# Cross attention's query and output projections as seven products of quarters, in an encoder-decoder kernel

## The chip, the core and the metric

The kernel runs on one core of a Trainium2 chip. The time is device microseconds of one launch. Everything is float32. Engines are called by the profile's names: PE (TensorE matmul), PEld (its weight loads), DVE (VectorE), ACT (ScalarE), POOL (GpSimd), SP (SyncE, which issues the transfers).

## What is computed

One layer of an encoder and a decoder, for a batch of 2. The source has 77 rows of 512 features, the target 2048; there are 16 heads of 32 and 2048 hidden features. The encoder's part is small. The decoder is:

```
yn = ln(y, n1);  y = y + mha(yn, yn, sa, causal and relative bias)
y = y + mha(ln(y, n2), memory, ca, relative bias)        # 77 keys
h = ln(y, n3);   y = y + relu(h @ ff1.T + b1) @ ff2.T + b2

mha:  q = (xq @ wq.T + bq);  k, v likewise from the other side, in 16 heads
      out = softmax(q k.T / sqrt(32) + bias) v;  return out @ w_out.T + b_out
```

The cross attention (`ca`) has two products with a 512 x 512 matrix on the target's side: the query projection and the output projection.

## The kernel before

The target's rows are worked in eight blocks of 512 (four per batch element), each of four tiles of 128 rows. There are three phases.

*Attention phase* (up to about 1740 us): self-attention in 128 units (batch, block, group of heads, tile). Small work is hung on lists by unit number: `light[n]` and `late[n]` hold functions that are called in unit n's slot. There the sums of the feed-forward's weights are prepared too (`w1_sums`, `w2_sums`): four loads of quarters into a scratch region `free`, sums and differences on POOL (`minus`, L1113), and a store into DRAM tensors `w1_d` and `w2_d`. The first block's cross attention (`first_cross`) is also hung there.

*Feed-forward with cross attention*: an outer loop over the eight blocks, x = 0 to 7. A block's feed-forward has `per` = 56 slots (`ff_slot`): 28 for the first matrix (`first_product`, matmuls at L1326, four of 128x256 per slot) and 28 for the second (`second_product`, matmuls at L1355, two products of four 128x128 matmuls per slot, and one in every fourth slot). Both matrices are already multiplied as seven products of quarters in place of eight: `ONE` and `TWO` list which left operand (a quarter or one of the sums S1 to S4) meets which right operand (a quarter or T1 to T4), into which of two accumulating chains of PSUM banks, and to which quarter of the result the chain's content then goes. The operand sums are made on the chip: `sums_n` makes T1 to T4 of the normalised input on POOL, all in slot 0; `sums_h` makes those of the hidden layer, on DVE (L1275, L1113, L1293) and POOL, four slots ahead of their use. Weight tiles of 256 KB stream through a ring of 16 (`w_ring`), which `feed` refills at the end of each slot; `next_w` takes the next tile.

Between the slots of block x-1's feed-forward stands the cross attention of block x (`cross(x)`, x = 1 to 7). It is a generator: `plan[n]` lists the steps of slot n, and before each `ff_slot` the loop calls `next(side)`. So the order on every engine is written out by hand: in each slot first the cross steps, then the feed-forward's.

The cross steps before, for tile t of a block:

- `norm_stages` n2: statistics in slot t (DVE, then POOL L767, L768), centring in t+2 (ACT L774; then POOL adds the output bias row to the residual y, L775), turning by PE in t+4 (L780), with ACT writing the scaled result (L783) into `nT2`.
- `q_group` in slots 9 to 12: 4 groups of 4 matmuls of 128x512 (L790) with weights resident in `w_q`, evacuated by DVE with bias and scale (L791).
- `attend_stages` at slot 14 + 7t: scores (L805, four banks, then on DVE a maximum L814 and a subtraction L815 for each bank, and with a relative bias an addition L812 before them), exponential 2 slots later (ACT L818), row sums (DVE L823) and normalising (POOL L829) 3 later, turning of the probabilities 6 later (16 transposes, L835, four banks; ACT copies L836), times values 9 later (L843; ACT copies to SBUF, L847), output projection 11 later (4 matmuls of 128x512, L852, and a DVE addition to y, L853). The first tile of a block starts one slot earlier.
- `norm_stages` n3, at 13, 15 and 17 slots after the tile's start, as above with the feed-forward's bias row.

Banks 0 to 3 of PSUM belong to the cross steps, in rotation (`bank()`); banks 4 to 7 are the feed-forward's chains (`pairs`).

*The last block's feed-forward* has no cross steps beside it.

Of the kernel before, what the change touches and what calls it, by code (L numbers as in the profile page):

```python
# [17 lines left out]
P = 128  # L18
# [36 lines left out]
def tile_encoder_decoder(ctx: ExitStack, tc: tile.TileContext, ins, out):  # L55
# [13 lines left out]
    make_identity(nc, ident)  # L69
    mhalf = const.tile([P, TB], F32, name="mhalf")  # L70
    nc.gpsimd.memset(mhalf, -0.5)
    vecs = const.tile([P, NVEC], F32, name="vecs")
# [85 lines left out]
    with (  # L158
# [597 lines left out]
        def norm_stages(y, n, row, place, done):  # L756
# [14 lines left out]
            def center():  # L771
                xn = keep["xn"] = place()
                rs = keep["rs"]
                nc.scalar.activation(xn, y(), AF.Identity, bias=rs[:, 2:3], scale=rs[:, 1:2])  # L774
                nc.gpsimd.tensor_tensor(y(), y(), row, ALU.add)  # L775

# [7 lines left out]

            return stats, center, turned

# [6 lines left out]
        def attend_stages(q, kTc, v, y, biased, pr, pts, place, w_o, bi=None):  # L793
# [44 lines left out]
            def times_v():  # L838
                ot = bank()
                for g in range(NC):  # L840
                    for r in range(HC):
                        h = g * HC + r
                        nc.tensor.matmul(  # L843
                            ot[rows4(r), ts(g, P)], v[:, ts(h, HD)], pts(g)[:, ts(r, P)], start=True, stop=True
                        )
                keep["oT"] = place()
                nc.scalar.copy(keep["oT"], ot)  # L847
# [6 lines left out]

            return score, exp, sums, normalize, turned, times_v, out

        def first_cross():
# [41 lines left out]
            for t in range(TB):  # L899
# [3 lines left out]
                )  # L903
                for k, f in enumerate(fs):
                    at(1 + t + k, f)
            for g in range(NC):
                at(7 + g, lambda g=g: q_group(g, wq[:, :, ts(g, P)], nT, qT[:, g, :]))
            for t in range(TB):
                y = lambda t=t: ys[t]
                fs = attend_stages(  # L910
                    lambda g, t=t: qT[:, g, ts(t, P)], kTc, vc, y, t < 2, prs[t % 2], pts, lambda: oT, wo
                )
# [3 lines left out]
                for k, f in enumerate(fs):  # L916
                    at(18 + 3 * t + k, f)
# [130 lines left out]
        oflat = oT_all.rearrange("p a q -> p (a q)")  # L1048
        pr = oflat[:, : H * S]
        kTcs = [pts_all[:, 4 + b, : NC * S].rearrange("p (c k) -> p c k", k=S) for b in range(B)]  # L1050
        w_q, vcs, qT = [], [], []

# [13 lines left out]
        def early_loads():  # L1066
            nc.sync.dma_start(nTt, nT3_d)
            row_into(bv, "dec_ca_out_b")
            for o in range(2):
                w_q.append(small_w(o * P, "dec_ca_in_wT"))  # L1070
            w_q.append(pts_all[:, 6, :].rearrange("p (c o) -> p c o", c=NC))

        def last_loads():
            t = sb.tile([P, MB], F32, name="q", tag="q", bufs=3)
            t = t.rearrange("p (c o) -> p c o", c=NC)
            nc.sync.dma_start(t, wchunk("dec_ca_in_wT", (NC - 1) * P, P))
            w_q.append(t)
            for b in range(B):
                t = sb.tile([P, MB], F32, name="q", tag="q", bufs=3)
                nc.sync.dma_start(t[:S, :], cv_d[:, b, :])  # L1080
                vcs.append(t)

        def late_loads():
            nc.sync.dma_start(w_q[2], wchunk("dec_ca_in_wT", 2 * P, P))
            for t in range(TB):
                new_y(1, t)
            for b in range(B):
                nc.sync.dma_start(kTcs[b], ckT_d[:, :, ts(b, S)])
            for _ in range(2):
                t = sb.tile([P, HC, 2 * P], F32, name="bias", tag="bias", bufs=2)  # L1090
                qT.append(t.rearrange("p (g a) k -> p g (a k)", g=2))

        light[len(units) - 5].append(early_loads)
        light[len(units) - 1].append(last_loads)


# [4 lines left out]
        w1_d = dram.tile([4, NC, P, D], F32, name="w1_d")  # L1101
        w2_d = dram.tile([7, 7, P, D], F32, name="w2_d")
        free = pp[:, 3 * HC * MB : END - 3 * HC * MB]
        tens = free.rearrange("p (z q o) -> p z q o", z=8, q=2)
# [56 lines left out]
        def w1_store(n):  # L1161
            nc.sync.dma_start(
                w1_d[:, n].rearrange("s p x -> p s x"), free[:, 4 * D :].rearrange("p (s x) -> p s x", s=4)
            )

        u = 2 * NU
        for c, k in enumerate((0, 2, 4, 10)):
# [37 lines left out]
        def w1_tile(name, n):  # L1205
# [4 lines left out]
            return ins["dec_ff1_wT"][c * TOK : (c + 1) * TOK, o : o + TOK].rearrange("(c p) o -> p c o", p=P)  # L1210

        def weight_tiles():
            for x in range(len(blocks)):
                for j, n in first_slots:
                    yield w1_tile(ONE[j][0], n)
                for _, name, _, _, _ in TWO:
                    for k in range(7):
                        yield w2_d[ON_W2[name], k]

# [27 lines left out]

        def sums_n():
            minus(gp, of_n("T1"), of_n("12"), of_n("11"))
            minus(gp, of_n("T2"), of_n("22"), of_n("T1"))  # L1250
            minus(gp, of_n("T3"), of_n("22"), of_n("12"))
            minus(gp, of_n("T4"), of_n("21"), of_n("T2"))

# [92 lines left out]
        def second_product(x, j, part):  # L1346
# [37 lines left out]
            elif done:  # L1384
                after[x * per + FIRST + 4 * j + 3 + 3] = store

        def ff_slot(s):
            x, n = divmod(s, per)
            if n == 0:
                sums_n()  # L1390
            k = n - FIRST + 4
# [10 lines left out]

        xt_ring, xt_turn = [pts_all[:, 7, :]], [0]

# [4 lines left out]
        def cross(x):  # L1409
# [9 lines left out]
            for t in range(TB):  # L1419
                fs = norm_stages(  # L1420
                    lambda t=t: y_of(x, t), "n2", bv, place("xt"), lambda t=t: nT2[:, :, ts(t, P)]
                )
                for k, f in zip((0, 2, 4), fs):
                    plan[t + k].append(f)
            for g in range(NC):
                plan[9 + g].append(lambda g=g: q_group(g, w_q[g], nT2, qT[g // 2][:, g % 2, :]))
            bias_1 = None
            if m == 0:

                spare = [pts_all[:, 4, :], vcs[0], y_of(x + 1, 0), y_of(x + 1, 1)]  # L1430
                bias_1 = [a[:, : NC * S].rearrange("p (g k) -> p g k", k=S) for a in spare]
                plan[3].append(lambda: bias_tile(pr.rearrange("p (h k) -> p h k", k=S), 2, P, S, 255))
                plan[5].append(lambda: [bias_tile(a, 2, P, S, 255 - P, r, HC) for r, a in enumerate(bias_1)])
            for t in range(TB):
                at = 14 + 7 * t
                y = lambda t=t: y_of(x, t)
                biased = m == 0 and t < 2
                fs = attend_stages(
                    lambda g, t=t: qT[g // 2][:, g % 2, ts(t, P)], kTcs[b], vcs[b][:S, :], y, biased, pr,
                    lambda g: pts_all[:S, g, :], place("xr"), wbt,  # L1440
                    bias_1 if biased and t else None,
                )
# [129 lines left out]
```

## Time and profile before

| | us |
|---|---|
| three runs, median (lowest to highest) | 2850.07 (2849.39 to 2850.22) |
| the profiled execution | 2851.01 |
| its span, from first to last instruction | 2849.2 |
| busy: PE, DVE, ACT, POOL | 2800.5, 1888.1, 1370.0, 836.7 |
| one block of the last phase with its cross attention (2340.20 to 2482.76) | 142.56 |

Views used below: the page's busy shares; the list of waits (who waited for whom: total us, number of times, longest); groups of instructions by line (count, busy time in all, mean ns of one); the timeline (start, length, engine, line, operation, out<-in, shape, count, and in brackets the idle time ahead of it and what ended it); the chain of work that ended last (start, length, engine, line, count); and busy time by windows. The length of a matmul record reaches into the next one, so the pace of a stream is read from the starts.

### The profile page before, as it was taken

The numbers are of one execution on the slowest core, as the hardware profiler recorded it, in microseconds if no ns is written. First come the engines' busy times: TensorE is split into PE (matmuls) and PEld (weight loads), VectorE is DVE, ScalarE is ACT, GpSimd is POOL, SyncE is SP. The second block draws the span as 40 slices with busy tenths as digits, with TensorE's granted clock in tenths as the row PEclk, the third lists the DMA queues.
The fourth block names the chain that finished last, engine by engine and source line by source line (L and its number), as shares of the span: only waits on it lengthen the run. The fifth ranks groups of instructions, "written<-read, shape, count | busy, mean of one in ns | idle before, by whom it ended". The sixth has DMA issues, their size and how long they took to land. (4 is left out here: it accounts for less than half of the span.)

```text
span 2849.2 us, 64689 instructions
## 1 busy us (share of the span) xinstructions
PE 2800.5 (98%) x25662; PEld 2020.5 (71%) x25662; DVE 1888.1 (66%) x5366; ACT 1370.0 (48%) x2583; POOL 836.7 (29%) x695
## 2 busy tenths in 40 slices
PE   9899999999999999999999999999999999999998
PEld 5557666666666456666666677888888888888888
DVE  4766687878886578788778894545454645454545
ACT  3444465546665446555556674333333333333331
POOL 0301143300100302121100002363636363636355
PEclk9899999999999999999999999999999999999999
DMA  6414343401112512232301115454546454545465
GB/s 172 123 46 140 119 140 106 129 23 49 36 50 65 141 39 71 81 106 78 98 20 43 44 34 191 137 178 135 180 136 197 134 181 135 180 135 180 120 203 181
DMA packets 262336, 324.55 MB, mean 114 GB/s; under 512 B 36192, under 2 KB 149392, under 8 KB 261906
## 3 DMA queue, kind: packets, MB, share of 16 engines
q1 hardware_dynamic: 262034, 320.42, 37.4%
q8 instruction: 202, 3.31, 0.5%
q14 instruction: 100, 0.82, 0.1%
HBM read 280.94 MB, written 39.40 MB: 112 GB/s over the span
## 5 line engine op out<-in xcount | busy, mean ns | idle before, releaser
L403 ACT ACTIVATE pp<-pp,nm 128x128 f32<-128x128 f32 (+15 forms) x512 | 611.7, 1201 | 258.9 <-DVE nm L398 258.6
L381 DVE TENSOR_SCALAR_CACHE_REDUCE pp<-psum 128x512 f32<-128x512 f32 (+3 forms) x1024 | 559.6, 591 | 63.1 <-PE psum L372 61.2
L426 PEld LDWEIGHTS psum<-ident,pp 128*128 128x128 f32 x4352 | 475.1, 142 | 106.2 <-DVE pp L381 50.8
L426 PE MATMUL psum<-ident,pp 128*128 128x128 f32 x4352 | 535.0, 278 | 7.0 <-ACT pp L403 3.7
L432 ACT COPY pts<-psum 128x512 f32<-128x512 f32 (+3 forms) x592 | 297.3, 575 | 457.3 <-PE psum L426 343.5
L430 DVE COPY pts<-psum 128x512 f32<-128x512 f32 (+2 forms) x544 | 330.0, 660 | 66.7 <-PE psum L426 66.3
L372 PE MATMUL psum<-kT,q 32*128 32x512 f32 (+3 forms) x2560 | 359.9, 576 | 5.2 <-ACT pts L432 2.6
L443 PEld LDWEIGHTS psum<-pts,vv 128*32 128x32 f32 x8704 | 226.2, 110 | 124.5 <-issue 116.6
L1355 PE MATMUL psum<-pp 128*128 128x128 f32 x2560 | 306.4, 276 | 1.9 <-POOL pp L1113 1.6
L1355 PEld LDWEIGHTS psum<-pp 128*128 128x128 f32 x2560 | 295.8, 192 | 17.4 <-issue 12.6
L443 PE MATMUL psum<-pts,vv 128*32 128x128 f32 x8704 | 279.4, 276 | 0.7 <-ACT pts L432 0.5
L1326 PE MATMUL psum<-vv,pp 128*128 128x256 f32 x1024 | 238.5, 381 | 0.0
L372 PEld LDWEIGHTS psum<-kT,q 32*128 32x128 f32 x2560 | 124.7, 183 | 141.5 <-issue 89.6
L1326 PEld LDWEIGHTS psum<-vv,pp 128*128 128x128 f32 x1024 | 189.8, 190 | 32.2 <-issue 8.4
L388 DVE CUSTOM_DVE_ANT_0 pp<-psum,bias 128x256 f32<-128x256 f32 (+1 forms) x512 | 196.0, 411 | 16.7 <-PE psum L372 16.5
L1113 POOL TENSOR_TENSOR pp<-pp 128x512 f32<-128x512 f32 x124 | 171.1, 1395 | 56.5 <-DMA pp<-in_dec_ff_wT_dram 53.5
L1342 ACT ACTIVATE kT<-kT,vecs 128x256 f32<-128x256 f32 x192 | 86.9, 499 | 192.1 <-DVE kT L1339 192.1
L1339 DVE TENSOR_TENSOR kT<-kT,psum 128x512 f32<-128x512 f32 x96 | 65.7, 685 | 169.8 <-PE psum L1326 96.9
L1326 PE MATMUL psum<-nT,pp 128*128 128x256 f32 x768 | 173.4, 379 | 0.0
L829 POOL TENSOR_TENSOR oT<-oT,cri 128x1232 f32<-128x1232 f32 x28 | 67.7, 2418 | 346.2 <-DVE cri L824 346.2
L1326 PEld LDWEIGHTS psum<-nT,pp 128*128 128x128 f32 x768 | 145.3, 190 | 28.6 <-issue 10.2
L285 POOL TENSOR_TENSOR rstd<-rstd,mhalf 128x1 f32<-128x1 f32 x32 | 18.5, 577 | 486.1 <-DVE rstd L284 424.4
(192 smaller groups left out, 3685.4 us busy)
## 6 DMA issues: line engine op xcount, KB each, us to landing
pp<-w_d SPq DMA_DIRECT2D x520, 256.0 KB
pp<-in_dec_ff_wT_dram SPq DMA_DIRECT2D x112, 256.0 KB
wqk<-in_dec_sa_in_wT_dram SPq DMA_DIRECT2D x64, 256.0 KB
bias<-tzg SPq DMA_DIRECT2D x128, 128.0 KB
wbig<-in_dec_sa_in_wT_dram SPq DMA_DIRECT2D x8, 1024.0 KB
vv<-in_enc_ff_wT_dram SPq DMA_DIRECT2D x8, 1024.0 KB
wbig<-in_dec_sa_out_wT_dram SPq DMA_DIRECT2D x8, 1024.0 KB
vv<-y SPq DMA_DIRECT2D x32, 256.0 KB
```

The lines of the kernel that those rows point to most:

```text
L372: nc.tensor.matmul(banks[r][:, : kn * P], q[rows4(r), ts(t, P)], kT[rows4(r), g, k0 * P : (k0 + kn) * P], start=True, stop=True,)
L381: nc.vector.tensor_scalar(p[:, k0 * P : (k0 + far) * P], s[:, : far * P], 1.0, None, ALU.mult, ALU.max, accum_out=st["mx"][:, r, c : c + 1],)
L388: nc.vector.tensor_tensor_reduce(p[:, (i + 1) * P - w : (i + 1) * P], s[:, far * P : kn * P], biases[b, m, g][:, r, 2 * P - w :], 1.0, LOW ...
L403: nc.scalar.activation(p, p, AF.Exp, bias=nm, accum_out=to)
L426: nc.tensor.transpose(pt[:, ts(x, P)], state[n]["p"][r][:, ts(k, P)], ident)
L430: nc.vector.tensor_copy(pts[:, : len(load), :], pt[:, :w])
L432: nc.scalar.copy(pts[:, : len(load), :], pt[:, :w])
L443: nc.tensor.matmul(ot[rows4(r), t, :], vv[:, k, ts(g * HC + r, HD)], got.pop((n, k, r)), start=(k == 0), stop=(k == i),)
L1113: engine.tensor_tensor(out, a, b, ALU.subtract)
L1326: nc.tensor.matmul(mm[:, ts(f, TOK)], a[:, c, ts(f, P)], b[:, c, :], start=fresh and f == 0 and c == 0, stop=c == 1, skip_group_check=True,)
L1342: nc.scalar.activation(dst[:, e, :], src[:, e, :], AF.Relu, bias=vec("dec_ff1_b", f + e))
L1355: nc.tensor.matmul(psum[:, bank_i, ts(col, P)], lhs[:, c, :], w[:, c, :], start=fresh and k in (0, 3) and c == 0, stop=c == 3, skip_group_ ...
```

## The change

- The query projection becomes seven products of quarters by the list `ONE`: four in weight quarters or sums of the weight (`wq_d`), with the T sums of `nT2` made on POOL (slots 8 and 9) into `n2_sums`. The products stand in slots 9 to 12 (2, 2, 2 and 1; `Q_SLOTS`), each of four matmuls of 128x256. Three results are added by DVE, four written by ACT (two activations of 128x256 each).
- The output projection is made for two tiles at a time: seven products of two matmuls of 128x256 in slots 30 to 32 and again in 39 to 41 (2, 2 and 3; `O_SLOTS`). The left operands are quarters of the two tiles' attention outputs and four sums of them (`sums_o`, with times values of the odd tile, slots 27 and 37); the sums' second-tile operands are read from the PSUM bank in place of its copy. Each product is followed by a DVE addition of 128x256 to y.
- The weight sums are prepared in the attention phase (`wc_sums`, `wc_store`, in units 7 and 8 of two blocks). Weight tiles for both projections go through the ring (`cross_tiles`: 7 tiles for the query, 4 for each pair of tiles of the output); `w_q` is gone, the raw quarters of the output weight stay resident.
- Tiles start at slot 13 + 5t, and all four with the same spacing inside. Probabilities get two buffers (`prs`), keys and values of one batch element are held at a time and replaced at the change of batch (`next_batch`).
- n3 stands at slots 33, 34, 42 and 43 (+0, +2, +4) for the four tiles. The addition of the bias row is a stage of its own: for n2 in slots 11 to 14, for n3 in slots 15 to 18 of the next block's feed-forward (`rows_later`).
- T1 to T4 of the feed-forward's input are made in slots 0, 1, 4 and 6 in place of all in slot 0.

The core of the diff:

```diff
-            for g in range(NC):
-                plan[9 + g].append(lambda g=g: q_group(g, w_q[g], nT2, qT[g // 2][:, g % 2, :]))
+            def q_product(j):
+                if j == 0:
+                    held["q"] = bank(), bank()
+                name, by, chain, fresh, to = ONE[j]
+                a, n, mm = next_w(2), of_n2(by), held["q"][chain]
+                for f in range(2):
+                    for c in range(2):
+                        nc.tensor.matmul(
+                            mm[:, ts(f, TOK)], a[:, c, ts(f, P)], n[:, c, :],
+                            start=fresh and f == 0 and c == 0, stop=c == 1, skip_group_check=True,
+                        )
...
+                if to in [p[4] for p in ONE[:j]]:
+                    nc.vector.scalar_tensor_tensor(dst, got, SCALE, dst, ALU.mult, ALU.add)
+                else:
+                    for f in range(2):
+                        nc.scalar.activation(
+                            dst[:, f, :], got[:, f, :], AF.Identity, bias=qbias[:, 2 * r + f : 2 * r + f + 1], scale=SCALE
+                        )
+            plan[8].append(lambda: [sum_n(n, of_n2) for n in ("T1", "T2")])
+            plan[9].append(lambda: [sum_n(n, of_n2) for n in ("T3", "T4")])
...
+            def sums_o(t):
+                s = {n: of_o(t, n) for n in ("S1", "S2", "S3", "S4", "11", "12", "21")}
+                a21, a22 = (held["o", t + 1]["bank"][:, ts(c, TOK)] for c in range(2))
+                minus(ve, s["S3"], s["11"], a21)
+                minus(ve, s["S2"], a22, s["S3"])
+                ve.tensor_tensor(s["S1"], s["21"], a22, ALU.add)
+                minus(gp, s["S4"], s["12"], s["S2"])
+
+            def o_product(t, j):
+                if j == 0:
+                    held["out"] = bank(), bank()
+                name, by, chain, fresh, to = ONE[j]
+                a, mm = of_o(t, name), held["out"][chain][:, :TOK]
...
+                for c in range(2):
+                    nc.tensor.matmul(
+                        mm, a[:, ts(c, P)], w[:, c, :], start=fresh and c == 0, stop=c == 1, skip_group_check=True
+                    )
+                d = y_of(x, t + int(to[0]) - 1)[:, ts(int(to[1]) - 1, TOK)]
+                ve.tensor_tensor(d, d, mm, ALU.add)
...
             for t in range(TB):
-                at = 14 + 7 * t
+                at = 13 + 5 * t
...
+                if t % 2:
+                    fs = fs[:5] + (lambda t=t, f=fs[5]: [f(), sums_o(t - 1)],)
-                for k, f in zip((0, 2, 3, 3, 6, 9, 11) if t else (-1, 1, 2, 3, 6, 9, 11), fs):
+                for k, f in zip((0, 2, 3, 3, 6, 9), fs):
                     plan[at + k].append(f)
                 fs = norm_stages(y, "n3", bo, place("xt"), lambda t=t: nTt[:, :, ts(t, P)])
-                for k, f in zip((13, 15, 17), fs):
+                at = (33, 34, 42, 43)[t]
+                for k, f in zip((0, 2, 4), fs):
                     plan[at + k].append(f)
+                rows_later[x * per + 15 + t] = fs[3]
...
+        Q_SLOTS = {9: (0, 1), 10: (2, 3), 11: (4, 5), 12: (6,)}
+        O_SLOTS = {at + k: js for at in (30, 39) for k, js in enumerate(((0, 1), (2, 3), (4, 5, 6)))}
...
-            if n == 0:
-                sums_n()
+            if n in (0, 1, 4, 6):
+                sum_n(f"T{(0, 1, 4, 6).index(n) + 1}", of_n)
```

`ONE` is not changed; a product's row is (left operand, right operand, chain, whether the chain starts afresh, quarter of the result):

```
("11", "11", 0, True, "11"), ("12", "21", 1, True, "11"), ("S2", "T2", 0, False, "12"),
("S1", "T1", 1, True, "22"), ("S3", "T3", 0, False, "22"), ("S4", "22", 1, False, "12"),
("22", "T4", 0, False, "21"),
```

More of the change, by code (lines that the diff above doesn't have):

```diff
@@ L845, in times_v @@
                         )
-                keep["oT"] = place()
+                keep["oT"], keep["bank"] = place(), ot
                 nc.scalar.copy(keep["oT"], ot)
@@ L853, in out @@
                 nc.vector.tensor_tensor(y(), mm, y(), ALU.add)
-            return score, exp, sums, normalize, turned, times_v, out
+            return score, exp, sums, normalize, turned, times_v, out, keep
         def first_cross():
@@ L1164, in w1_store, with quarter, wc_sums, wc_store @@
             )
+        def quarter(name, r, c):
+            return ins[name][r * TOK : (r + 1) * TOK, c * TOK : (c + 1) * TOK].rearrange("(c p) o -> p c o", p=P)
+        def wc_sums(name, turned):
+            z = free.rearrange("p (z k o) -> p z k o", z=8, k=2)
+            q = {}
+            for i, (r, c) in enumerate(((0, 0), (0, 1), (1, 0), (1, 1))):
+                nc.sync.dma_start(z[:, i], quarter(name, c, r) if turned else quarter(name, r, c))
+                q[r, c] = z[:, i]
+            s1, s2, s3, s4 = (z[:, 4 + i] for i in range(4))
+            if turned:
+                gp.tensor_tensor(s1, q[1, 0], q[1, 1], ALU.add)
+                minus(gp, s2, s1, q[0, 0])
+                minus(gp, s3, q[0, 0], q[1, 0])
+                minus(gp, s4, q[0, 1], s2)
+            else:
+                minus(gp, s1, q[0, 1], q[0, 0])
+                minus(gp, s3, q[1, 1], q[0, 1])
+                minus(gp, s2, q[1, 1], s1)
+                minus(gp, s4, q[1, 0], s2)
+        def wc_store(dst):
+            nc.sync.dma_start(
+                dst.rearrange("s p x -> p s x"), free[:, 4 * D :].rearrange("p (s x) -> p s x", s=4)
+            )
+        for u, name, turned, dst in (
+            (2 * NU, "dec_ca_in_wT", True, wq_d), (6 * NU, "dec_ca_out_wT", False, wo_d)
+        ):
+            light[u + 7].append(lambda name=name, turned=turned: wc_sums(name, turned))
+            late[u + 8].append(lambda dst=dst: wc_store(dst))
         u = 2 * NU
```

113 lines of the change are left out of this document (79 added, 34 removed).

## The prediction

> **What bounds the kernel now.** I read first the busy shares of the page, then the waits of PE from 1500 us on, then one block of the last phase (the feed-forward of block x-1 in 56 slots, with the cross attention of block x put between them) in the view by windows: stretch, its length, then busy time of PE, PEld, DVE, ACT and POOL.
>
> ```profile
> PE 2800.5 (98%) x25662; PEld 2020.5 (71%) x25662; DVE 1888.1 (66%) x5366; ACT 1370.0 (48%) x2583; POOL 836.7 (29%) x695
> ...
> PE psum L780 <- ACT xt L774: 7.0, 12, 1.1
> PE psum L780 <- ACT pts L774: 3.5, 6, 1.1
> PE psum L1355 <- POOL pp L1113: 1.6, 2, 1.2
> ...
> 2340.20:2482.76 142.56, 140.79 (x1033) 115.65 (x1033) 75.53 (x134) 54.58 (x116) 73.66 (x61) 1.00 0.50 157
> ```
>
> PE sets the end, at granted clock 1.00. A block costs 142.56 us and PE idles 1.77 us of it; the first two waits (10.5 us in 18 cases, three in each of six blocks) are that idle time. So a matmul taken away is worth its full time, and each new wait costs its full length.
>
> **Matmuls.** The two projections run at these lines; below them how closely they follow each other.
>
> ```profile
> L852 PE MATMUL psum<-wbig,xr 128*128 128x512 f32 x224 | 100.7, 592 | 0.0
> ...
> L790 PE MATMUL psum<-pp,wqk 128*128 128x512 f32 x112 | 50.4, 592 | 0.0
> ...
> 2197.47 3.60 PE L790 MATMUL psum<-pp,wqk 128*128 128x512 f32 x8
> 2200.90 1.89 PE L1326 MATMUL psum<-vv,pp 128*128 128x256 f32 x8
> ...
> 2748.18 48.35 PE psum L1326 x224
> ```
>
> Each matmul is two records. A block has 16 + 16 of them, 512 wide, so 64 records; eight take 3.43 us (2197.47 to 2200.90): 27.44 us. The L1326 stream has the shape of the new products, 128x256: 48.35/224 = 0.2158 us a record. After: 7 products of four matmuls for the query, 14 of two for the output, 112 records, 24.17 us. Saved: 3.27 us a block, in 7 blocks **-22.9 us**. A rule that speaks against halving the width is in the Trainium skill, "TensorE: Matmul & The Clock Gate", section "Back-to-back issue gap": in a stream of weight loads and matmuls it gives about 81 ns at width 128 and 131 ns at 512, so half the width costs more than half. Interpolated, that is an estimate of 0.75 of the price for half the width: 35.8 us for the 112 records and +59 us in all for this term. The stream above pays 0.50; the trace decides.
>
> **The waits of L780.** They stand in slots 4 to 7 (pairs are start and length; brackets are idle time).
>
> ```profile
> 2179.11 1.28 POOL L1374 TENSOR_TENSOR vv<-vv,oT 128x512 f32<-128x512 f32 x1 [4.98 <-DVE oT L1371]
> ...
> 2185.02 1.27 POOL L1113 TENSOR_TENSOR vv<-nT,vv 128x512 f32<-128x512 f32 x1
> 2186.25 0.55 POOL L767 TENSOR_TENSOR crs<-crs,mhalf 128x1 f32<-128x1 f32 x1
> ...
> 2187.19 0.81 ACT L774 ACTIVATE xt<-vv,crs 128x512 f32<-128x512 f32 x1 [2.36 <-POOL crs L768]
> ...
> 2185.09 1.89 PE L1326 MATMUL psum<-vv,pp 128*128 128x256 f32 x8
> 2188.05 0.66 PE L780 MATMUL psum<-ident,xt 128*128 128x128 f32 x4 [1.07 <-ACT xt L774]
> ...
> 2188.71 1.48 ACT L783 ACTIVATE pp<-psum,vecs 128x128 f32<-128x128 f32 x4
> 2190.08 0.81 ACT L774 ACTIVATE pts<-vv,crs 128x512 f32<-128x512 f32 x1
> 2190.78 0.58 ACT L1336 COPY kT<-psum 128x512 f32<-128x512 f32 x1
> 2191.24 1.52 ACT L783 ACTIVATE pp<-psum,vecs 128x128 f32<-128x128 f32 x4
> ```
>
> Four sums of 1.27 us stand in POOL's queue ahead of the second tile's statistics (L767), which the centring and so the transposes await. After, one sum goes into each of slots 0, 1, 4 and 6, and the row additions, 1.27 us each, leave slots 2 to 5. POOL's order becomes: residual to 2180.4, statistics, T1, statistics, T2 at about 2184.6, needed at 2185.09: it just fits. Next in line is ACT: 2.53 us a tile (2188.71 to 2191.24) against PE's 1.73 + 0.43 a slot. With its lead from the earlier statistics it falls about 0.1 us behind at the last tile. **-10.5 + 0.7 = -9.8 us**; bounds -10.5 and -7 (T2 late by 0.5 us in each block).
>
> **A new wait: transposes behind scores.** Tiles now start every five slots, not seven: score(t+1) stands in slot 18+5t, the turning of tile t in 19+5t, one feed-forward slot between. Both take all four side banks in the same turn, so each of the four groups of transposes waits until DVE has read the matching bank twice (the built program has one DVE wait a group). Before, turning came ahead of the score.
>
> ```profile
> 2360.77 1.13 PE L805 MATMUL psum<-pts,bias 32*128 32x77 f32 x32
> 2361.83 1.99 PE L1326 MATMUL psum<-vv,pp 128*128 128x256 f32 x8
> 2363.66 7.07 PE L1326 MATMUL psum<-nT,pp 128*128 128x256 f32 x32
> ...
> 2374.02 1.91 PE L835 MATMUL psum<-ident,oT 128*77 128x128 f32 x16
> 2375.76 1.89 PE L1326 MATMUL psum<-vv,pp 128*128 128x256 f32 x8
> ...
> 2362.43 0.48 DVE L815 TENSOR_TENSOR oT<-psum,cmx 128x308 f32<-128x308 f32 x1
> ...
> 2365.13 0.48 DVE L815 TENSOR_TENSOR oT<-psum,cmx 128x308 f32<-128x308 f32 x1
> ...
> 2369.20 2.25 POOL L829 TENSOR_TENSOR oT<-oT,cri 128x1232 f32<-128x1232 f32 x1 [31.82 <-DVE cri L824]
> ...
> 2398.38 2.05 PE L1355 MATMUL psum<-pp,kT 128*128 128x128 f32 x16
> ...
> 2401.82 0.48 DVE L815 TENSOR_TENSOR oT<-psum,cmx 128x308 f32<-128x308 f32 x1
> ...
> 2219.26 1.99 PE L1326 MATMUL psum<-vv,pp 128*128 128x256 f32 x8
> ...
> 2223.60 0.47 DVE L812 TENSOR_TENSOR oT<-psum,oT 128x308 f32<-128x308 f32 x1
> ```
>
> From the score's end (2361.83): the slot's product ends at +1.83, the four groups (1.74/4 = 0.435 us each) want to start at 1.83, 2.27, 2.70 and 3.14 and to end at 3.57. The banks are free at +1.08 to +3.78 in steps of 0.90; in the second score (2398.38) the last at +3.92. Groups three and four wait: the last ends at 4.27 to 4.48, 0.70 to 0.91 late. I take 0.84, since most scores run behind a queue like the second's. Three a block, 21 in all; in one of them the score adds a bias tile (L812, which frees the bank): the last bank comes at +4.8 (2224.07 less 2219.26), its group of 0.435 and some ends at 5.37, and the wait is 1.8. 20 x 0.84 + 1.8 = **+18.6 us**. Bounds: nothing, and 3.92 - 1.83 = 2.1 us each (44 us) if the first group waited for the last bank. That the normalised tile is late instead is no danger: 10.7 us from 2360.77 to the end of L829, against 1.06 + 1.83 + 4 x 1.73 + 1.06 + 1.83 = 12.7 us in the first tile's six new slots.
>
> **A second one: the output's seventh product.** In slots 32 and 41 products 4, 5 and 6 follow each other; 6 goes into 4's bank, whose sum DVE must first have added.
>
> ```profile
> 2405.71 1.42 DVE L823 TENSOR_REDUCE csu<-oT 128x16 f32<-128x1232 f32 x1
> ...
> 2407.34 0.36 DVE L1369 TENSOR_TENSOR oT<-psum,oT 128x256 f32<-128x256 f32 x1
> 2407.74 0.43 DVE L1370 TENSOR_TENSOR oT<-psum,oT 128x256 f32<-128x256 f32 x1
> 2408.08 0.28 DVE L1371 TENSOR_TENSOR oT<-psum,oT 128x128 f32<-128x128 f32 x1
> ...
> 2304.86 8.93 PE psum L1355 x80
> ...
> L1113 DVE TENSOR_TENSOR pp<-pp,kT 128x512 f32<-128x512 f32 x32 | 50.8, 1627 | 0.0
> ...
> 2397.32:2434.13 36.81, 36.81 (x370) 31.91 (x369) 33.28 (x51) 12.57 (x26) 28.79 (x20) 1.00 0.64 198
> ```
>
> In slot 31 DVE's list is: add 3, row sums of the last tile (1.63 us from 2405.71 to 2407.34), three mixing adds (1.02), then add 4 (0.42, as L1370 of the same size): about 3.65 us after product 3. PE has eight L1355 records (0.89) and products 4 and 5 (0.86 each) for that time, 2.62. It waits 1.05 us: x7 = **+7.4**. In slot 41 no row sums stand there, two half sums do: 0.2 us, **+1.4**. Bounds: nothing, and 1.6 us a place if a half sum (1.63) stands ahead.
>
> **What is hidden.** The products' evacuations, 8 activations on ACT and 3 + 14 adds on DVE with 6 operand sums in place of 8 passes, end no wait elsewhere: in slots 28 to 40 (the window above) DVE was busy 33.28 of 36.81 us; after, one score (3.7), one row sum (1.7) and a statistics leave that stretch and 11 adds and 3 operand sums of 0.42 come: about as much work, in 39 us. On sums with both inputs in SBUF, DVE takes 1.63 us where GpSimd works beside it. The Trainium skill, "GPSIMD Engine Reference", section "1. Specifications", gives the reason, an SBUF interface shared with DVE instructions of two SBUF inputs; the adds that read PSUM would then keep 0.42 beside it, as L1370 does. Were they stretched by the same factor, each of them would cost DVE 0.4 us more, and so the slow rival would start. The two preparations of weight sums on POOL (slots 7 of blocks 2 and 6 of the attention phase, four sums each) have a slot of over 10 us before the next tile's centring. Fifteen more weight tiles a block go through the ring:
>
> ```profile
> 2796.53:2847.00 50.47, 44.80 (x393) 43.88 (x391) 29.59 (x45) 2.70 (x9) 39.34 (x27) 1.00 0.61 194
> ```
>
> The last block drew 194 GB/s here and the window above 198, and no PE wait names a transfer; the query's tiles, 256 KB per product of 1.73 us, are 152 GB/s. I take nothing.
>
> **Sum.** -22.9 - 9.8 + 18.6 + 7.4 + 1.4 = -5.3 us. The profiled execution took 2851.01; after, 2845.7. The three runs' median is 2850.07, 0.94 below: **2844.7 us**.
>
> **Rivals.** *The bank waits are nothing*: the groups find their banks read, if DVE gets through a score faster than these rows. For it: nothing but that no such wait exists in before. -5.3 - 18.6: 2826. *The seventh product does not wait*, because add 4 comes in time (a shorter list in slot 31): -5.3 - 8.8, 2836. *Slower: DVE is late for the output's products.* Its adds queue behind half sums of 1.63 us; for it speaks 90% busy in the window above; against it, that turning and score waits give DVE time. It decides when the add of product 0 comes later than 1.7 us after product 1 ends, which is the slot that lies before product 2. Two extra waits of about 1.1 us a block: +15, 2860. *The ring or a sum late*: 1 to 2 us a block, 2852 to 2859. *Half the width costs more than half*: if 256 wide pays 0.52 of 512, as L1355's 128 wide does of 256 (8.93/80 = 0.112 of 0.216), 0.8 us a block is lost and 2850.3 comes out; the stream at 0.2158 speaks against it. The Trainium skill's section named above would go further that way.
>
> **How the numbers follow.** The sum's own case 0.58, own range 2840 to 2850; banks nothing 0.10; no seventh wait 0.11; DVE late 0.13; ring or sum 0.06; matmuls 0.02. 0.2% is 5.7 us (about what a measurement of this kernel can tell from no change), so the limits are 2844.4 and 2855.8, and the sum's case lies on the first: half of it, 0.29, counts as faster, 0.29 as the same. Faster 0.29 + 0.10 + 0.11 = 0.50; same 0.29 + 0.02 + 0.02 = 0.33; slower 0.13 + 0.04 = 0.17. The range 2829 to 2858 leaves out the first rival and the worst part of the third.
>
> **What would show it.** In the profile after: 392 + 392 records of 128x256 at 0.216 us in the two projections; no wait of the n2 transposes above 0.2 us; waits of the turning transposes on DVE's subtraction, 0.7 to 0.9 us a tile in 21 tiles; 7 waits of the output's product on its add, near 1 us. Wrong would be: those waits absent, half sums or weights named in PE's waits, or records above 0.22 us.

## The result and the profile after

| | before | after |
|---|---|---|
| median (lowest to highest), 4 runs each | 2850.14 (2849.39 to 2851.57) | 2835.36 (2833.69 to 2838.43) |
| ratio to before, 95% interval | | 0.9952 (0.9939 to 0.9965) |
| the profiled execution; its span | 2851.01; 2849.2 | 2836.94; 2835.0 |

The kernel is 14.8 us faster; the forecast was 5.4 us (2844.7, range 2829 to 2858). The sign and the main mechanisms were right, the size was short by 9.4 us.

Lines are renumbered after: L780 is now L783, L805 L808, L814 and L815 are L817 and L818, L823 L826, L835 L838, L843 L846, L847 L850, L1326 L1376, L1355 L1405; the query's matmuls are L1493, the output's L1536, its additions L1540.

First PE's row of the busy shares, then PE's waits in the last phase (total us, times, longest), then one block in the view by windows (stretch, length, busy PE, PEld, DVE, ACT, POOL, clock, DMA share, GB/s):

```profile
PE 2783.7 (98%) x25998; PEld 2079.9 (73%) x25998; DVE 1896.0 (67%) x5472; ACT 1396.0 (49%) x2639; POOL 874.1 (31%) x745
```

```profile
PE psum L1536 <- DVE vv L1540: 5.5, 7, 0.8
PE psum L838 <- DVE pts L818: 3.1, 13, 0.2
PE psum L838 <- DVE oT L818: 1.7, 7, 0.2
...
PE psum L838 <- DVE pts L815: 1.5, 2, 0.8
...
PE psum L783 <- ACT q L775: 0.2, 1, 0.2
```

```profile
2330.30:2470.54 140.24, 138.54 (x1081) 124.38 (x1080) 76.75 (x149) 58.31 (x124) 77.45 (x68) 1.00 0.59 188
```

The waits of the n2 transposes are gone but for one of 0.2 us, and the two new waits stand where the forecast put them: the seventh product behind the addition of product 4, whose bank it takes, and the turning behind the score's bank reads. A block takes 140.24 us, 2.32 less than before; over seven blocks that would be 16.2 us, more than the phase gains below, mostly because only six blocks had the n2 stalls and one pays for a score with a bias tile.

**An account by lines.** The idle column leaves out part of a stall (shown below), so I use another sum: each group of matmuls in PE's timeline is given the time from its start to the start of the next group, except that idle time listed ahead of a group is given to the group that waits, and these are added by line from the first feed-forward record of the last phase to the end of the span. The columns after "after" are experiments described below.

| us in the last phase | before | after | n2 moves alone | turning later | seventh apart | both | score in 29 | output 512 |
|---|---|---|---|---|---|---|---|---|
| query projection | 96.1 | 84.6 | 96.1 | 84.6 | 84.6 | 84.6 | 84.6 | 84.6 |
| output projection | 96.2 | 92.8 | 96.2 | 92.8 | 85.4 | 85.4 | 85.4 | 96.2 |
| n2, n3 transposes | 36.0 | 25.7 | 24.8 | 25.4 | 25.7 | 25.4 | 25.4 | 25.4 |
| score | 29.7 | 30.6 | 29.7 | 39.2 | 30.7 | 39.2 | 29.7 | 29.7 |
| turning | 49.3 | 65.6 | 49.3 | 49.2 | 65.6 | 49.2 | 49.2 | 55.4 |
| context | 28.3 | 28.3 | 28.3 | 28.3 | 28.3 | 28.3 | 28.3 | 28.3 |
| feed-forward, first | 394.7 | 395.4 | 392.5 | 395.4 | 395.4 | 395.3 | 394.7 | 395.3 |
| feed-forward, second | 366.4 | 361.6 | 366.3 | 361.6 | 361.5 | 361.6 | 362.3 | 367.9 |
| two more lines, which no edit touches | 14.2 | 14.2 | 14.2 | 14.2 | 14.2 | 14.2 | 14.2 | 14.2 |
| whole phase | 1111.0 | 1098.8 | 1097.5 | 1090.6 | 1091.4 | 1083.1 | 1073.8 | 1097.0 |

Of the 14.2 us between the two spans, 12.2 lie in this phase. The other 2.0 lie ahead of it: its first record comes at 1738.21 before and at 1736.20 after. Over all twelve profiles of this study that start scattered from 1735.4 to 1738.6 with no order by the edits, so I don't count it to the change; the last section shows one source of it.

### The profile page after: what moved, and what is told of

Its sections match the earlier page's. It is cut to its first block, busy times and chain, and to the rows that moved or that the text cites. A ratio compares the mean times of both kernels' runs of the same rounds, so it can differ in the third digit from the quotient of the medians.

```text
span 2835.0 us, 65811 instructions
## 1 busy us (share of the span) xinstructions
PE 2783.7 (98%) x25998; PEld 2079.9 (73%) x25998; DVE 1896.0 (67%) x5472; ACT 1396.0 (49%) x2639; POOL 874.1 (31%) x745
## 5 line engine op out<-in xcount | busy, mean ns | idle before, releaser
L1405 PE MATMUL psum<-pp 128*128 128x128 f32 x2560 | 303.8, 276 | 1.9 <-POOL pp L1113 1.6
L1405 PEld LDWEIGHTS psum<-pp 128*128 128x128 f32 x2560 | 295.8, 192 | 6.8 <-issue 2.4
L1113 POOL TENSOR_TENSOR pp<-pp 128x512 f32<-128x512 f32 x159 | 204.9, 1305 | 118.5 <-DMA pp<-in_dec_ff_wT_dram 53.6
L1376 PE MATMUL psum<-vv,pp 128*128 128x256 f32 x1024 | 239.9, 383 | 0.0
L1376 PEld LDWEIGHTS psum<-vv,pp 128*128 128x128 f32 x1024 | 189.2, 190 | 27.8 <-issue 1.9
L1376 PE MATMUL psum<-nT,pp 128*128 128x256 f32 x768 | 172.3, 379 | 0.0
L1376 PEld LDWEIGHTS psum<-nT,pp 128*128 128x128 f32 x768 | 144.8, 190 | 19.3 <-issue 0.2
L472 POOL TENSOR_TENSOR oT<-rirows,oT 128x512 f32<-128x512 f32 x30 | 38.6, 1287 | 356.5 <-DMA rirows<-rec 356.5
```

The lines of the kernel that those rows point to most:

```text
L1113: engine.tensor_tensor(out, a, b, ALU.subtract)
L1376: nc.tensor.matmul(mm[:, ts(f, TOK)], a[:, c, ts(f, P)], b[:, c, :], start=fresh and f == 0 and c == 0, stop=c == 1, skip_group_check=True,)
L1405: nc.tensor.matmul(psum[:, bank_i, ts(col, P)], lhs[:, c, :], w[:, c, :], start=fresh and k in (0, 3) and c == 0, stop=c == 3, skip_group_ ...
```

## The experiments

**The n2 waits alone.** Is the removed wait worth 9.8 us, and which of the two moves removes it? Three kernels made from the one before; the first has both hunks, the second only the sums' (slots 0, 1, 4 and 6), the third only the row additions' (a stage `add` of its own, at t + 11):

```diff
-            if n == 0:
-                sums_n()
+            if n in (0, 1, 4, 6):
+                sum_n(f"T{(0, 1, 4, 6).index(n) + 1}", of_n)
...
-                nc.gpsimd.tensor_tensor(y(), y(), row, ALU.add)
+                if n == "n3":
+                    add()
...
-                for k, f in zip((0, 2, 4), fs):
+                for k, f in zip((0, 2, 4, 11), fs):
                     plan[t + k].append(f)
```

> The kernel before, with only the four weight-free operand sums of the feed-forward spread over slots 0, 1, 4 and 6 and the second normalisation's row additions moved seven slots on. The forecast's term for this was -9.8: 2840.3. Account by lines of the two profiles (the transposes' own line -10.2, the feed-forward stream beside them -2.2, less 0.7 that moved with the 32-row steps): about -13: 2837 (2836 to 2839). Rival, the waits went for another reason in the changed kernel, such as the new order of the tiles, which this kernel does not have: 2848 or more.

> The kernel before with only the feed-forward's operand sums spread over slots 0, 1, 4 and 6; row additions stay in slots 2 to 5. If the sums in front of the second tile's statistics are the whole cause: 2838 to 2839, all of what both together gave. If the additions matter as much (each 1.27 us in GpSimd's list, ahead of the fourth tile's statistics): 2843 to 2846.

> The kernel before with only the row additions of the second normalisation moved seven slots on; the four operand sums stay in slot 0. If the sums are the cause, little comes: 2846 to 2849. If the additions are: 2840 or less.

Measured: both 2837.54 (0.9955 of before, 0.9943 to 0.9968); sums alone 2836.71 (0.9953, 0.9938 to 0.9968); row additions alone 2848.94 (1.0001, 0.9992 to 1.0010). By the medians of the runs beside them that is 11.7, 12.7 and 0.4 us. In the waits of the kernel with the row additions alone, the old rows are all there (L784 is its line of the transposes):

```profile
PE psum L784 <- ACT xt L774: 7.1, 12, 1.1
PE psum L784 <- ACT pts L774: 3.6, 6, 1.1
```

So the spread of four sums of 1.27 us earns all of it, and the row additions nine slots later (the expectations say seven) earn nothing. Without them the third tile's statistics do come earlier on POOL (they end at 2328.80), but ACT takes that tile's centring only at 2330.85, behind its work on the second tile: what counts is the second tile's delay, and that one the four sums set. The gain is 1111.0 - 1097.5 = 13.5 us, not 9.8. Why more than its idle time is seen in the timeline of before (start, length, ..., count, idle ahead) and of the kernel with both moves (L784 and L1329 there):

```profile
2327.23 0.60 PE L780 MATMUL psum<-ident,pts 128*128 128x128 f32 x4
2327.66 1.89 PE L1326 MATMUL psum<-vv,pp 128*128 128x256 f32 x8
2330.62 0.66 PE L780 MATMUL psum<-ident,xt 128*128 128x128 f32 x4 [1.06 <-ACT xt L774]
2331.11 1.89 PE L1326 MATMUL psum<-vv,pp 128*128 128x256 f32 x8
```

```profile
2320.88 0.60 PE L784 MATMUL psum<-ident,pts 128*128 128x128 f32 x4
2321.32 1.89 PE L1329 MATMUL psum<-vv,pp 128*128 128x256 f32 x8
2323.05 0.60 PE L784 MATMUL psum<-ident,xt 128*128 128x128 f32 x4
2323.48 1.89 PE L1329 MATMUL psum<-vv,pp 128*128 128x256 f32 x8
2325.21 0.60 PE L784 MATMUL psum<-ident,xt 128*128 128x128 f32 x4
2325.65 1.89 PE L1329 MATMUL psum<-vv,pp 128*128 128x256 f32 x8
2327.50 0.65 PE L784 MATMUL psum<-ident,pts 128*128 128x128 f32 x4
2327.99 3.62 PE L1329 MATMUL psum<-vv,pp 128*128 128x256 f32 x16
```

From a transpose group to the slot after the next one takes 2331.11 - 2327.23 = 3.88 us with the stall and 2323.48 - 2320.88 = 2.60 without: 1.28 us for a wait that shows 1.06. The rest is the end of the last record ahead, which is hidden in the next one only while the stream runs on (2330.62 - 1.06 - 2327.66 = 1.90 against 1.73), and a slower pass of the stalled group (0.49 against 0.43). Over the 18 stalls (slot and transposes, 53.5 us against 18 x 2.164 = 39.0 unstalled) the cost is 14.6 us, 4.1 more than the 10.5 of idle time, 0.23 each. And 1.1 us of it stays after the moves: in the last four rows the fourth tile's transposes come 1.85 us after the slot's start in place of 1.73 and then take 0.49, in each of the six blocks. So short an idle time is not listed. 14.6 - 1.1 = 13.5.

**The turning one slot later.** Is the turning's extra time the read of the score's banks?

```diff
-                for k, f in zip((0, 2, 3, 3, 6, 9), fs):
-                    plan[at + k].append(f)
+                for k, f in zip((0, 2, 3, 3, 7, 9), fs):
+                    plan[at + k].insert(0 if k == 7 else len(plan[at + k]), f)
```

> The changed kernel with each tile's turning one slot later (20+5t in place of 19+5t; in slot 30 ahead of the output's products). Account by lines of the two profiles: the turning's line took 17 us more in the last phase than before, because its four groups wait for DVE's reads of the score's banks. With one more feed-forward slot (1.73 us) between score and turning, the turning starts 3.56 us after the score's end, where the last bank comes free at 3.8 to 3.9, so no group waits: 2835.4 - 16 = 2819 (2817 to 2822). Rival, DVE is simply behind: its work moves by the same time, and the wait comes back at the context product, the row sums or the output's products; then at most half is won, 2827 or more.

Measured: 2827.37 (2826.00 to 2827.96), 0.9922 of before (0.9909 to 0.9936): 8.0 us better than the changed kernel, half of what was expected. The turning's line does fall by 16.4 us (65.6 to 49.2), about the 16 that was expected. But the score's line rises by 8.6: a wait that the stall had covered. PE's waits in that kernel, and the place:

```profile
PE psum L808 <- DVE wqk L1522: 6.7, 7, 1.0
PE psum L1536 <- DVE vv L1540: 5.5, 7, 0.8
```

```profile
2378.97 0.46 PE L808 MATMUL psum<-pts,bias 32*128 32x77 f32 x6
2380.37 1.08 PE L808 MATMUL psum<-pts,bias 32*128 32x77 f32 x26 [0.95 <-DVE wqk L1522]
```

The score of the last tile, in slot 28, needs the bank of tile 1's context (slot 27), and the output's operand sums read that bank on DVE. That the turning waited for the banks holds; that no wait comes behind it was wrong. The rival's number (2827 or more) is the measured one, and so is its half; its reason fits in part only, since DVE is not behind in general: the wait comes back at this one place.

**The seventh product in a slot of its own.**

```diff
-        O_SLOTS = {at + k: js for at in (30, 39) for k, js in enumerate(((0, 1), (2, 3), (4, 5, 6)))}
+        O_SLOTS = {30: (0, 1), 31: (2, 3), 32: (4, 5), 33: (6,), 39: (0, 1), 40: (2, 3), 41: (4, 5, 6)}
```

> The changed kernel with the seventh output product of the first pair of tiles in a slot of its own (33) in place of following products 4 and 5 in slot 32. Account by lines: that product waits about 1.1 us a block for the add of product 4, in 7 blocks 7.5 us; a slot of 1.8 us covers it: 2835.4 - 7.5 = 2828 (2826 to 2830). Rival, the statistics of the third normalisation, which follow in slot 33 and need the seventh sum, become late and give the time back: 2834 to 2836.

Measured: 2829.97 (2829.14 to 2832.44), 0.9934 (0.9921 to 0.9946), 5.4 us below the changed kernel; by the account the output's line falls by 7.4 (92.8 to 85.4), the phase by 7.3, and nothing else moves by more than 0.1. That 5.4 and 7.3 differ lies within the scatter between executions.

**Both.**

> Both edits: turning a slot later and the seventh product in slot 33. If the two waits are independent, 2835.4 - 16 - 7.5 = 2812 (2809 to 2815). If DVE is the limit behind both, the second edit brings little beyond the first: 2819 to 2827.

Measured: 2821.74 (2820.95 to 2822.08), 0.9903 (0.9887 to 0.9918); 13.6 us below the changed kernel. The phase falls by 15.7, within 0.2 of the sum of the two edits alone (8.2 + 7.3): the two waits are independent, and the new wait of the score stands unchanged (39.2). The 2812 of the expectation had priced the first edit at 16.

**Who holds the score's bank?** DVE's list and then ACT's in the kernel with both edits, ahead of the score, which starts at 2375.88 and stops after six records, where it comes to the bank of the context:

```profile
2373.76 1.44 DVE L826 TENSOR_REDUCE csu<-oT 128x16 f32<-128x1232 f32 x1 [1.74 <-ACT oT L821]
...
2375.94 0.41 DVE L1113 TENSOR_TENSOR wqk<-xr,psum 128x256 f32<-128x256 f32 x1
...
2376.73 0.41 DVE L1522 TENSOR_TENSOR wqk<-xr,psum 128x256 f32<-128x256 f32 x1
```

```profile
2372.48 1.24 ACT L821 ACTIVATE oT<-oT 128x1232 f32<-128x1232 f32 x1
...
2375.13 0.58 ACT L850 COPY xr<-psum 128x512 f32<-128x512 f32 x1
```

A row sum stands in DVE's list ahead of the operand sums and waits for an exponential (L821) that ACT does behind the turning's copies. Two kernels attack that chain at its two ends; each starts from the kernel with both edits.

```diff
-                    plan[at + k].insert(0 if k == 7 else len(plan[at + k]), f)
+                    plan[at + k].insert(0 if k in (2, 7) else len(plan[at + k]), f)
```

> The kernel with both edits (turning a slot later, seventh product in slot 33), and now the next tile's exponential ahead of the turning's copies in ScalarE's queue. In the kernel with both edits a new wait stood before the last score, 0.95 us in each of 7 blocks (6.6 us, and 1.9 us more in that line's records): its banks are read by the output's operand sums, which stand in DVE's list behind a row sum, which waits for that exponential. With the exponential first the row sum comes some 2 us earlier and the wait goes: 2821.7 - 8 = 2814 (2812 to 2816). Rival, the copies of the turning, now 1.25 us later, delay the context product by as much in three tiles a block: 2821 to 2840.

```diff
-                for k, f in zip((0, 2, 3, 3, 7, 9), fs):
+                for k, f in zip((0, 2, 4, 4, 7, 9) if t == 2 else (0, 2, 3, 3, 7, 9), fs):
```

> The kernel with both edits, and tile 2's row sum behind the operand sums in DVE's list (a slot later) in place of ahead of them. With both edits the row sum ended at 2375.5, and the operand sums ran 2375.94 to 2377.14; ScalarE's copy of the context, which the sums read, ended at 2375.71. So only 0.2 us a block can be won, since the copy is as late as the row sum: 2820 to 2822. Rival, the row sum alone is the cause: 2814.

Measured: exponential first 2821.53 (2819.91 to 2822.54), no gain; row sum after 2819.10 (2816.39 to 2821.72), 2.6 us by the medians and 0.8 by the phase. In the first, the row sum does come earlier, and the wait is now named after ACT:

```profile
PE psum L808 <- ACT kT L1392: 4.2, 7, 0.6
```

```profile
2375.97 0.42 DVE L1113 TENSOR_TENSOR wqk<-xr,psum 128x256 f32<-128x256 f32 x1 [1.55 <-ACT xr L850]
```

DVE now stands idle for 1.55 us until ACT's copy of the context (L850) has ended; with the exponential in front that copy became 0.22 us later (it starts at 2375.35 in place of 2375.13), and by the same account the context, turning and output lines grew by 2.6 us while the score's fell by 2.5, as the rival had it. The operand sums end no earlier (2377.17, against 2377.14). My expectation had followed one chain of two that end within 0.3 us of each other (DVE free at 2375.94, ACT's copy done at 2375.71). The second kernel's expectation, made from both lists, was near: 0.8 us by the phase where 1.4 was expected.

**More room in place of a shorter chain.** The last tile's score goes from slot 28 to 29, and what follows it moves a slot:

```diff
+        O_SLOTS = {31: (0, 1), 32: (2, 3), 33: (4, 5), 34: (6,), 40: (0, 1), 41: (2, 3), 42: (4, 5, 6)}
...
+                at = (13, 18, 23, 29)[t]
...
+                for k, f in zip((0, 2, 3, 3, 8, 10) if t == 2 else (0, 2, 3, 3, 7, 9), fs):
+                    plan[at + k].insert(0 if k in (7, 8) else len(plan[at + k]), f)
...
+                at = (34, 35, 43, 44)[t]
```

> The kernel with both edits, and the last tile's score in slot 29 in place of 28, with what follows it a slot later too (turning of tile 2 in 31, its context in 33, the first output products in 31 to 34, the second in 40 to 42, third statistics in 34, 35, 43 and 44). Now two feed-forward slots lie between tile 1's context and the score whose bank it holds. If the new wait of the kernel with both edits is the read of that bank (ScalarE's copy and DVE's operand sums end 1.1 us after the score wants to start), it goes whole, with the stretched records beside it: 2821.7 - 8.5 = 2813 (2811 to 2816). Rival: the shifted products or the statistics find a queue of their own and give it back: 2819 to 2823.

Measured: 2812.57 (2809.81 to 2816.43), 0.9875 of before (0.9860 to 0.9889), the fastest version here, 22.8 us below the changed kernel (25.0 by the phase). The score's line is back at 29.7. In the list of waits of the last phase only rows of the last block's feed-forward are left, and between score and turning nothing idles:

```profile
PE psum L1405 <- POOL pp L1113: 1.6, 2, 1.2
PE psum L1405 <- DVE pp L1113: 0.3, 1, 0.3
```

```profile
2371.81 1.13 PE L808 MATMUL psum<-pts,bias 32*128 32x77 f32 x32
2372.87 3.84 PE L1405 MATMUL psum<-pp 128*128 128x128 f32 x32
2376.54 1.91 PE L838 MATMUL psum<-ident,oT 128*77 128x128 f32 x16
```

**Is the output's half of the change worth anything where it was put?** The changed kernel with the output projection of before (at 11 slots after the tile's start), all else kept:

```diff
-        O_SLOTS = {at + k: js for at in (30, 39) for k, js in enumerate(((0, 1), (2, 3), (4, 5, 6)))}
+        O_SLOTS = {}
...
-                for k, f in zip((0, 2, 3, 3, 6, 9), fs):
+                for k, f in zip((0, 2, 3, 3, 6, 9, 11), fs[:7]):
```

> The changed kernel with the output projection back at four matmuls of 512 a tile (two slots after the context, as before; no operand sums for it, no tiles of its weight sums in the ring), all else as changed. Account by lines: +11.45 for the matmuls, -7.4 for the seventh product's wait; and the product of tiles 0 and 1, 1.72 us, now falls between the score and the turning of the second and third tile, where it covers their bank waits: -(0.83 + 0.63) x 7 = -10.2. Together 2835.4 - 6.2 = 2829 (2827 to 2832). So the output's quarters as placed would be worth nothing. Rival, the waits are independent of what stands between, and only the products count: 2839.

Measured: 2834.79 (2833.59 to 2836.27), 0.9948 (0.9935 to 0.9960): the same as the changed kernel. The turning's line falls by 10.2 us (65.6 to 55.4), the very number expected: the wide product between score and turning covers the bank wait, as its rows show (a score at 2372.90, a slot, the product, the turning at its unstalled 1.74):

```profile
2373.97 1.99 PE L1376 MATMUL psum<-vv,pp 128*128 128x256 f32 x8
2375.80 3.60 PE L855 MATMUL psum<-wbig,xr 128*128 128x512 f32 x8
2379.23 1.91 PE L838 MATMUL psum<-ident,pts 128*77 128x128 f32 x16
2380.97 3.62 PE L1376 MATMUL psum<-nT,pp 128*128 128x256 f32 x16
```

The expected total was 5.8 us too low (4.4 by the phase), since the second feed-forward product's line grew by 6.3. Seven new waits of 0.3 us for half sums, 2.2 us, and some 1.9 us of stretch around them are the largest part; before, this group had two cases:

```profile
PE psum L1405 <- POOL pp L1113: 3.8, 9, 1.2
```

Another 0.6 us is a context that now stands next to a feed-forward slot; 1.6 us I did not follow. So the output's seven products, as placed in this change, are worth nothing against four wide ones: their matmuls save 10.8 us and their place brings 7.4 and 10.2 of waits, while the wide ones bring these 6.3 of their own. With the two waits moved out of the way (score in 29) their line keeps the full 10.8 us; the wide products were not run in that order.

## Why the prediction was right in sign and short in size

**Matmuls: -22.9 forecast, -22.3 read.** Query 96.1 to 84.6 is -11.5; output, without its wait, 96.2 to 85.4 is -10.8 (with the seventh product apart). The pace:

```profile
2330.30 3.62 PE L1493 MATMUL psum<-pp 128*128 128x256 f32 x16
2333.76 1.89 PE L1376 MATMUL psum<-vv,pp 128*128 128x256 f32 x8
```

Sixteen records in 3.46 us, 0.216 each, as the feed-forward's stream had said. The Trainium skill's two figures for the spacing in a stream ("TensorE: Matmul & The Clock Gate", section "Back-to-back issue gap"), between which the forecast interpolated an estimate of 0.75 of the price for half the width, do not carry over to this float32 stream: it pays 0.50 (0.216 against 0.429).

**Waits of L780: -9.8 forecast, -13.5 read.** This is the step that failed most, and it failed in size: it took the 10.5 us of the idle column for the worth of the stalls, which was 14.6. The 0.7 that it took off for ACT's lag is there as 1.1, at the last tile, as it said; the list shows 0.2 of it, in one case. That T2 just fits was right: in the block above it ends on POOL at 2319.30 and PE takes it at 2319.81. The row additions, which the forecast moved together with the sums, were no part of the cause.

**Turning: +18.6 forecast, +16.3 read** (and 0.9 in the score's line, which come with the operand sums: in the kernel without them, "output 512", that line is at 29.7). The rows of one tile, to be read as the forecast did, from the score's end:

```profile
2373.95 1.99 PE L1376 MATMUL psum<-vv,pp 128*128 128x256 f32 x8
2375.78 1.84 PE L838 MATMUL psum<-ident,pts 128*77 128x128 f32 x12
2377.85 0.66 PE L838 MATMUL psum<-ident,pts 128*77 128x128 f32 x4 [0.24 <-DVE oT L818]
2378.35 3.62 PE L1376 MATMUL psum<-nT,pp 128*128 128x256 f32 x16
```

From 2375.78 to 2378.35 are 2.57 us against 1.74: 0.83 late, where 0.84 was taken; the block's other two tiles were 0.76 and 0.64 late, and the tile behind the score with a bias tile 1.98, where 1.8 was taken. Only 0.24 of it shows as idle time; the third group's stall lies inside the x12 row. Who looks for the forecast's "0.7 to 0.9 us a tile" in the list of waits alone would call it wrong by a factor of three.

**Seventh product: +7.4 and +1.4 forecast, +7.4 read.** PE's rows and DVE's list, which is the one that the forecast wrote down:

```profile
2400.81 1.03 PE L1536 MATMUL psum<-wbig,wqk 128*128 128x256 f32 x4
2402.62 1.13 PE L1536 MATMUL psum<-pp,xr 128*128 128x256 f32 x4 [0.79 <-DVE vv L1540]
2403.68 1.08 PE L846 MATMUL psum<-pts,q 77*32 77x128 f32 x32
```

```profile
2399.25 0.42 DVE L1540 TENSOR_TENSOR vv<-vv,psum 128x256 f32<-128x256 f32 x1 [0.44 <-PE psum L1536]
2399.59 1.43 DVE L826 TENSOR_REDUCE csu<-pts 128x16 f32<-128x1232 f32 x1
...
2402.16 0.74 DVE L1540 TENSOR_TENSOR vv<-vv,psum 128x256 f32<-128x256 f32 x2
```

Row sum, three mixing adds, then add 4. Product 6 (the seventh; they are counted from 0) could have started at 2400.81 + 0.86 = 2401.67 and starts at 2402.62: 0.95 late, 6.7 us in seven blocks, and some 0.1 a block more in its own slower pass. The forecast had 1.05 of waiting alone, so that the sums agree to a tenth is partly luck. In slot 41 nothing waits; that 1.4 us was not there.

**Hidden at nothing: -1.0 read.** The terms so far make -22.3 - 13.5 + 16.3 + 0.9 + 7.4 = -11.2 of the phase's -12.2; 1.0 is left. The two feed-forward lines move by more (+2.9 and -4.7 against the kernel with the n2 moves alone), but most of that is only a change of place: a feed-forward group next to a score or context takes 0.1 us longer on that side (1.83 from 2373.95 to 2375.78 above, behind a score, against 8 x 0.216 = 1.73), and with tiles that start earlier 28 such sides moved into the first product, 42 left the second, and the other 14 stand against other side steps. What is left, under 1 us, I did not follow. No listed wait in the last phase names a weight tile, and the additions that read PSUM kept 0.42 us, as forecast.

Together: the n2 term gained 3.7 us more than forecast, the turning cost 1.4 less (with the score's share), the output's waits 1.4 less, the matmuls gained 0.6 less, the rest gained 1.0: 6.9 of the 9.4 us. The 2.0 ahead of the phase lie within the scatter named above.

**The rivals.** *Bank waits nothing*: false (16.3 us). *The seventh product does not wait*: its time, 2836, is the measured one, but its mechanism is false; the wait is there in all seven blocks. A time that fits is no proof of the case that gave it. *DVE late for the output's products* and *ring or sum late*: not seen as a wait in the changed kernel; but DVE's late operand sums did appear as soon as the turning's stall no longer covered them. *Half the width costs more than half*: false (0.50).

## What to carry to other kernels

Price a stall, taken away or added, by the time from start to start over the whole group against an unstalled group of the same shape; the idle column of a pipelined engine understates it, here by 0.23 us for each of 18 stalls, and for the turning by two thirds. When steps are packed closer and share rotating buffers, count for each step the slots between the last reader of its buffer and its own start: one slot of 1.7 us was too little here for banks that DVE needed 3.9 us to read, two were enough, and moving a few steps by a slot each was worth 1.5 times the change itself (22.8 us against 14.8). And when one wait is removed, look for the second chain that ends within a few tenths of it before promising the gain.

## What the runs showed of the hardware

Executions of one kernel differed by 1 to 9 us. One reason stands in the rows of the window from 630 to 640 us, in which every kernel here does the same work; first before, then after (the 0.66 and the 1.00 are the granted clock, a mean over the 10 us):

```profile
620.00:630.00 10.00, 8.44 (x119) 6.29 (x120) 7.93 (x22) 3.65 (x6) 1.28 (x1) 1.00 0.49 133
630.00:640.00 10.00, 10.00 (x38) 6.83 (x39) 8.41 (x32) 2.42 (x4) 0.00 (x0) 0.66 0.01 2
```

```profile
630.00:640.00 10.00, 10.00 (x44) 5.88 (x45) 9.28 (x33) 4.32 (x6) 0.00 (x0) 1.00 0.01 2
```

PE had been busy 8.44 of the 10 us ahead of that in both, and its longest listed idle time there was 1.23 us. In nine of twelve profiles the clock then fell (before: to 0.50, from 633.27 to 640.10 us), in three (the changed kernel's among them) it stayed at 1.00, with the same instructions. The two profiles are level ahead of it (the same group of matmuls starts at 626.03 before and 626.07 after); behind it a group starts at 643.67 before and at 641.19 after, 2.5 us earlier. That is more than the 2.0 us at the start of the last phase; the 0.5 that goes the other way I did not follow. Nor is the clock the whole of the scatter: the turning a slot later, with the fall, reaches the last phase first of all (1735.44), the row sum after, without it, only at 1737.64.

What sets off the fall no run here shows. The Trainium skill ("TensorE: Matmul & The Clock Gate", section "What's actually happening") says that the window in which the clock's gate watches PE runs free of the program, so that the same program may meet it at another phase; a fall in nine of twelve profiles of the same instructions is in keeping with that, but shows no such window.
